# Attention's output: scattered to feature rows by DMA and divided there, in place of two rounds of transposes

## The chip, the cores and the metric

The kernel runs on one core of a Trainium2 chip. The core has a matrix engine (TensorE, "PE" in the profile, with its weight loads as "PEld"), a vector engine (VectorE, "DVE"), a scalar engine (ScalarE, "ACT"), a general engine (GpSimd, "POOL"), and SyncE ("SP"), whose queue issues DMAs. Each engine takes its instructions in program order and waits in that order. The metric is device time in microseconds of one launch; the median of the runs counts.

## The reference, cut to what matters

A sequence of 2048 tokens with 256 features passes through attention, a gated MLP, a second attention, and the same MLP again, each with a layer norm ahead and a residual sum behind. Both attentions are causal and have 16 heads of 16 features; the first has rotary angles and four key heads, the second has 16 key heads. The MLP has 2048 inner features, with weights in 4-bit codes.

```python
probs = softmax(where(causal, q @ k.T * scale, -inf))   # per head, 2048 x 2048
attended = (probs @ v).reshape(S, 256)                  # heads side by side: 16 x 16 features
x = x + attended @ Wo.T + bo                            # the second attention has no bo
x = x + mlp(layernorm(x))
```

The change lies between `probs @ v` and `attended @ Wo.T`.

## The kernel before, in words

Queries are tiled in four blocks `b` of 512 tokens (TB), heads in four groups `g` of four. A unit is one (b, g): 16 units per attention, in the order b = 0: g = 0 to 3, then b = 1, and so on. The number of key tiles grows with the block: 4(b + 1) tiles of 128 keys.

**A unit's main steps** come from `value_steps`. `pair(kt, p)` computes scores with keys on partitions for two heads (L716), adds minus the row maximum (L721) and the mask (L628), and ScalarE takes the exponential (L729). `values(half)` multiplies by V (L703) into one PSUM tile `av`: each of the four heads has 32 rows of it, of which 16 are the output features and row 16 is the softmax sum, since V has a column of ones. `end()` copies `av` to `o` in SBUF on ScalarE (L739).

**A unit's side steps** are woven between the main ones. `max_steps` computes the next unit's scores with queries on partitions (L643) and VectorE takes their maxima (L651); `gather` and `turn` bring them into the form that L721 needs. In g = 0 and g = 1 the preparation of the next block is added (`prep_steps`); in the first attention also the unpacking of the MLP's weights, six steps per unit from block 1 on (`dequant_steps`: a load on SP's queue, L314, a POOL step L328, VectorE steps L339 to L354).

**Division and projection.** `divide` of a unit is the first side step of the next one. Four transposes (L746) turn `o` to tokens on partitions, VectorE takes the reciprocal of the sums (L751) and multiplies (L754) into `att`. At the start of the next block, `out_steps` transposes `att` back to feature rows (`turn`, L775), ScalarE copies it to `aT` (L780), and `project` multiplies with `wo` (L787) and adds to `x` (L792). After the last unit of an attention the divide and the out steps become side steps of the MLP's first block (`left`), woven between its `features` steps (L876 on TensorE, L882 to L887 on the others).

**Order.** Nothing is scheduled automatically: every engine's order is the program's. `weave(main, side, rest=4)` spreads the side list evenly over the main steps but the last four; `blend` merges two lists evenly. PSUM has three score tiles `ps_s`, used in turn by pairs, scores and the MLP's features, one `ps_av` and one `ps_m`, which divides, turns and projections share.

**SP's queue** carries, per unit, the eight DMAs of `load_q` for the unit after next (L614), stores of prepared queries and keys (L535, L539), loads of packed weights, and ahead of each MLP the 2 MB load of the down weights `wd` (L868). `load_q` is emitted at the beginning of a unit, ahead of its weave.

Of the kernel before, what the change touches and what calls it, by code (L numbers as in the profile page):

```python
# [8 lines left out]
F32 = mybir.dt.float32  # L9
# [7 lines left out]
ALU = mybir.AluOpType  # L17
# [3 lines left out]
P = 128  # L21
S = 2048
D = 256
NH = 16
HD = 16
NKV = 4
NG = NH // 4
MLP = 2048
NFC = MLP // P
TB = 512  # L30
NB = S // TB
NT = TB // P
# [23 lines left out]
def blend(a, b):  # L56

    keyed = [((n + 0.5) / len(a), 0, n, f) for n, f in enumerate(a)]
    keyed += [((n + 0.5) / len(b), 1, n, f) for n, f in enumerate(b)]
    return [f for *_, f in sorted(keyed, key=lambda k: k[:3])]  # L60
# [3 lines left out]
def tile_hybrid_layers(  # L64
# [25 lines left out]
    nc = tc.nc  # L90
# [9 lines left out]
    small = ctx.enter_context(tc.tile_pool(name="small", bufs=2))  # L100
    pre = ctx.enter_context(tc.tile_pool(name="pre", bufs=1))
    psum = ctx.enter_context(tc.tile_pool(name="psum", bufs=1, space=PSUM))
    dram = ctx.enter_context(tc.tile_pool(name="dram", bufs=1, space=bass.MemoryType.DRAM))
# [7 lines left out]
    def ps_m():  # L111
        return psum.tile([P, 512], F32, tag="m", name="ps_m")
# [36 lines left out]
    for src, at in ((bq, 0), (bk, D), (bv, D + 64)):  # L149
        n = src.shape[1]  # L150
# [18 lines left out]
    ident = const.tile([P, P], F32, tag="ident", name="ident")  # L169
# [221 lines left out]
    class Attention:  # L391
# [293 lines left out]
        def value_steps(self, b, g):  # L685

            nk = NT * (b + 1)
            held = {"pending": []}

            def values(half):  # L690

                kt, q0, es_ = held["pending"][0]
                few = TB - q0 <= TB // 2
                if half == 1:
                    held["pending"].pop(0)
                    if few:
                        return
                elif kt == 0:
                    held["av"] = ps_av()
                own = slice(q0, TB) if few else slice(*((q0, TB // 2), (TB // 2, TB))[half])  # L700
                for j in range(4):
                    h = g if self.first else 4 * g + j
                    nc.tensor.matmul(  # L703
                        held["av"][32 * j : 32 * j + 32, own],
                        lhsT=self.vv[kt // NT][:, kt % NT, h * VW : h * VW + 32],
                        rhs=es_[j // 2][:, j % 2, own],
                        start=(kt == 0 and half == 0), stop=(kt == nk - 1),
                    )

            def pair(kt, p):  # L710
                q0 = max(0, kt - NT * b) * P
                diagonal = kt >= NT * b
                keys = slice((kt % NT) * P, (kt % NT + 1) * P)
                pt = ps_s()
                for r in range(2):
                    nc.tensor.matmul(  # L716
                        pt[:, r, q0:], lhsT=self.key_rows(kt // NT, g, p, r, keys),
                        rhs=self.qT[b, g][64 * r : 64 * r + 64, p, q0:], start=True, stop=False,
                    )
                for r in range(2):  # L720
                    nc.tensor.matmul(  # L721
                        pt[:, r, q0:], lhsT=sel[64 * r : 64 * r + 64, p, :],
                        rhs=self.mT[b, g][64 * r : 64 * r + 64, q0:],
                        start=False, stop=not diagonal,
                    )
                if diagonal:
                    self.add_mask(pt, 1, q0)
                e = self.wk.tile([P, 2, TB], F32, tag="e", name="e", bufs=4)
                nc.scalar.activation(e[:, :, q0:], pt[:, :, q0:], AF.Exp, scale=QK_SCALE)  # L729
                if p == 0:  # L730
                    held["es"] = [e]
                else:
                    held["pending"].append((kt, q0, held["es"] + [e]))

            def end():
                values(0)
                values(1)
                o = pre.tile([P, TB], F32, tag="o", name="o")
                nc.scalar.copy(o, held["av"])  # L739
                held["o"] = o  # L740

            def divide():
                o = held["o"]
                pt = ps_m()
                for i in range(NT):
                    nc.tensor.transpose(  # L746
                        pt[:, i * P : (i + 1) * P], o[:, i * P : (i + 1) * P], ident
                    )
                heads = pt.rearrange("p (t j c) -> p t j c", t=NT, c=32)
                rec = small.tile([P, NT, 4], F32, tag="rec", name="rec")  # L750
                nc.vector.reciprocal(rec, heads[:, :, :, HD])  # L751
                if g == 0:
                    self.att[b] = pre.tile([P, NT, NG, 4, HD], F32, tag="att", name="att")
                nc.vector.tensor_tensor(  # L754
                    self.att[b][:, :, g], heads[:, :, :, :HD],
                    rec.unsqueeze(3).broadcast_to([P, NT, 4, HD]), ALU.mult,
                )

            steps = []
            for kt in range(nk):  # L760
                for p in range(2):
                    steps.append(lambda kt=kt, p=p: pair(kt, p))
                    if kt:
                        steps.append(lambda p=p: values(p))
            return steps, end, divide

        def out_steps(self, b):
            held = {}

            def turn(n):  # L770
                pt = ps_m()
                for i in range(2):
                    flat = self.att[b][:, 2 * n + i].rearrange("p g j c -> p (g j c)")
                    for c in range(2):
                        nc.tensor.transpose(  # L775
                            pt[:, (2 * i + c) * P : (2 * i + c + 1) * P],
                            flat[:, c * P : (c + 1) * P], ident,
                        )
                aT = pre.tile([P, 2, 2, P], F32, tag="aT", name="aT")
                nc.scalar.copy(aT, pt.rearrange("p (i c t) -> p i c t", i=2, c=2))  # L780
                held[n] = aT

            def project(n):
                po = ps_m()
                for i in range(2):
                    for c in range(2):
                        nc.tensor.matmul(  # L787
                            po[:, i * D : (i + 1) * D], lhsT=held[n][:, i, c, :],
                            rhs=self.wo[:, c, :], start=(c == 0), stop=(c == 1),
                        )  # L790
                to = xt[b][:, 2 * n : 2 * n + 2, :]
                nc.vector.tensor_tensor(  # L792
                    to, po.rearrange("p (i d) -> p i d", i=2), to, ALU.add
                )

            return [lambda n=n, f=f: f(n) for n in range(2) for f in (turn, project)]

        def run(self, extra, beside):


            units = [(b, g) for b in range(NB) for g in range(NG)]
            per_unit = -(-len(extra) // (len(units) - NG))
            late, ahead = [], []
            for n, (b, g) in enumerate(units):
                more = []
                if g == 0 and b > 0:
                    more += self.out_steps(b - 1)
                if g == 0 and b + 1 < NB:
                    ahead = self.prep_steps(b + 1)
                    few = -(-len(ahead) // 2)  # L810
                if n >= NG:
                    more, extra = more + extra[:per_unit], extra[per_unit:]
                if g < 2:
                    more, ahead = more + ahead[:few], ahead[few:]
                if n + 2 < len(units):
                    self.load_q(*units[n + 2])
                steps, turn = [], None
                if n + 1 < len(units):
                    steps, turn = self.max_steps(*units[n + 1])
                else:  # L820
                    more += beside
                side = late + (blend(steps, more) if steps else more)
                steps, end, divide = self.value_steps(b, g)
                weave(steps, side, rest=4)
                if turn:
                    turn()
                end()
                late = [divide]
            return late + [lambda: None] * 2 + self.out_steps(NB - 1)


    class Mlp:
# [89 lines left out]
    at = Attention(True, wqkv_a)  # L922
    with tc.tile_pool(name="wk1", bufs=2) as wk, tc.tile_pool(name="kv1", bufs=1) as kv:
        at.wk = at.qpool = wk
        with tc.tile_pool(name="init", bufs=1) as pool:
# [13 lines left out]
            steps, turn = at.max_steps(0, 0)  # L939
# [5 lines left out]
    at = Attention(False, wqkv_b)  # L945
    with tc.tile_pool(name="kv20", bufs=1, reuse_waits="tile") as kv0, tc.tile_pool(
        name="wk2", bufs=2, reuse_waits="tile"
# [7 lines left out]
        steps, turn = at.max_steps(0, 0)  # L955
# [60 lines left out]
```

## Time and profile before

| | |
|---|---|
| time, median of 3 runs (lowest to highest) | 1926.59 us (1915.77 to 1930.18) |
| the profiled execution, its own time | 1916.85 us |
| its span, from the first to the last instruction | 1914.7 us |
| mean granted TensorE clock | 0.979 |
| TensorE busy | 1829.9 us (96%) |
| VectorE, ScalarE, GpSimd busy | 1109.2, 813.5, 238.0 us (58%, 42%, 12%) |
| DMA queues of SP (q1), share of 16 engines | 8.5% |
| L746 transposes, 128 | 22.2 us busy on TensorE |
| L775 transposes, 64 | 11.1 us busy on TensorE |
| L751 and L754 on VectorE, 32 each | 8.2 and 13.6 us |
| L780 copies on ScalarE, 16 | 9.3 us |
| units' ends (copies `o`): first attention | 69.9 to 646.6 us |
| units' ends: second attention | 1024.7 to 1568.0 us |

The page's first part gives each engine's busy time and its share of the span; the clock row has one digit per fortieth of the span, 9 for nine tenths of full clock or more. In the timeline each row is a run of equal instructions of one engine: start and duration in us, engine, line, operation, output and input tiles, shapes, count, and in brackets the idle time ahead of it and what ended it. The end of a TensorE instruction is modelled and overlaps the next start; starts are what can be subtracted.

### The profile page before, as it was taken

Reading aid. Unit: us, or ns where it says so; the run is one execution under the profiler, and the core shown is the slowest. Engines: PE = TensorE matmul, PEld = TensorE weight load, DVE = VectorE, ACT = ScalarE, POOL = GpSimd, SP = SyncE. Lnnn points to the kernel's source line nnn. Section 1 sums busy time; section 2 is a strip of 40 time slices with the busy share of each in tenths; the row PEclk is TensorE's granted clock in tenths of the full one; section 3 lists DMA queues with packets and bytes.
Section 4 is the critical chain, followed back from the end, with each engine's and each line's share of the span. In section 5 each row is a group of like instructions: output and inputs, shape, how many; then the busy total and the mean of one; then the engine's idle time right before and its main releaser. Section 6 shows DMA issues by size and latency. Waiting matters only on the chain. (4 is left out here: it accounts for less than half of the span.)

```text
span 1914.7 us, 31770 instructions
## 1 busy us (share of the span) xinstructions
PE 1829.9 (96%) x13452; PEld 985.9 (51%) x13452; DVE 1109.2 (58%) x1612; ACT 813.5 (42%) x1069; POOL 238.0 (12%) x433
## 2 busy tenths in 40 slices
PE   5899989999999999999999999999999999999999
PEld 3454444444444456656565545445444444756656
DVE  4556677787776253444444667766867715363443
ACT  1334445465666521222214355556556662131221
POOL 3301311300001011112102010010000001011110
PEclk8879999999999999999999899999999999999999
DMA  4510320301101100002305050050000010000000
GB/s 102 131 45 23 72 46 23 73 23 23 34 23 34 45 6 0 1 0 47 75 1 111 24 100 23 13 100 23 13 13 1 2 46 0 11 1 11 6 6 11
DMA packets 42270, 64.23 MB, mean 34 GB/s; under 512 B 13840, under 2 KB 20880, under 8 KB 41872
## 3 DMA queue, kind: packets, MB, share of 16 engines
q1 hardware_dynamic: 33488, 45.93, 8.5%
q0 software_dynamic: 7680, 15.74, 5.1%
q8 instruction: 106, 1.74, 0.4%
q10 hardware_dynamic: 960, 0.52, 0.1%
q14 instruction: 36, 0.29, 0.1%
HBM read 44.24 MB, written 17.83 MB: 32 GB/s over the span
## 5 line engine op out<-in xcount | busy, mean ns | idle before, releaser
L729 ACT ACTIVATE e<-ps_s 128x1024 f32<-128x1024 f32 (+3 forms) x640 | 571.5, 897 | 457.8 <-PE ps_s L628 227.8
L651 DVE TENSOR_REDUCE mx<-ps_s 128x2 f32<-128x1024 f32 (+3 forms) x640 | 657.9, 1061 | 171.0 <-PE ps_s L643 85.9
L703 PE MATMUL ps_av<-e,v 128*32 128x256 f32 (+1 forms) x4608 | 363.9, 383 | 0.7 <-ACT e L729 0.7
L643 PE MATMUL ps_s<-kT,qT 64*128 64x512 f32 (+3 forms) x1280 | 281.8, 436 | 31.3 <-DVE mx L651 12.2
L716 PE MATMUL ps_s<-qT,kT 64*128 64x512 f32 (+3 forms) x1280 | 289.9, 449 | 11.4 <-DVE mx L651 6.1
L876 PE MATMUL ps_s<-xnT,wg 128*128 128x512 f32 x512 | 242.5, 596 | 0.0
L721 PE MATMUL ps_s<-mT,sel 64*128 64x512 f32 (+3 forms) x1280 | 240.9, 372 | 0.2 <-ACT mT L677 0.2
L876 PE MATMUL ps_s<-xnT,wu 128*128 128x512 f32 x512 | 240.6, 592 | 0.0
L643 PEld LDWEIGHTS ps_s<-kT,qT 64*128 64x128 f32 x1280 | 124.3, 187 | 186.1 <-issue 85.4
L716 PEld LDWEIGHTS ps_s<-qT,kT 64*128 64x128 f32 x1280 | 122.3, 187 | 158.6 <-issue 80.9
L884 DVE TENSOR_TENSOR t<-ps_s,t 128x512 f32<-128x512 f32 x128 | 88.2, 689 | 171.2 <-POOL t L883 169.4
L882 ACT ACTIVATE t<-ps_s 128x512 f32<-128x512 f32 x128 | 76.3, 596 | 249.9 <-PE ps_s L876 249.5
L885 ACT ACTIVATE t<-t 128x512 f32<-128x512 f32 x128 | 80.6, 630 | 201.2 <-DVE t L884 201.2
L703 PEld LDWEIGHTS ps_av<-e,v 128*32 128x32 f32 x4608 | 92.7, 108 | 136.6 <-issue 113.4
L876 PEld LDWEIGHTS ps_s<-xnT,wu 128*128 128x128 f32 x512 | 97.3, 190 | 122.5 <-issue 122.5
L883 POOL TENSOR_SCALAR t<-t 128x512 f32<-128x512 f32 x128 | 79.4, 620 | 577.7 <-ACT t L882 574.9
L876 PEld LDWEIGHTS ps_s<-xnT,wg 128*128 128x128 f32 x512 | 96.2, 192 | 106.4 <-issue 104.5
L886 DVE SCALAR_TENSOR_TENSOR t<-t,ps_s 128x512 f32<-128x512 f32 x128 | 88.1, 688 | 89.0 <-ACT t L885 89.0
L721 PEld LDWEIGHTS ps_s<-mT,sel 64*128 64x128 f32 x1280 | 124.5, 190 | 10.0 <-ACT mT L677 6.5
L628 PE MATMUL ps_s<-mask_t,mask_w 64*128 64x64 bf16 x2048 | 125.1, 199 | 0.0
L901 PE MATMUL ps_av<-wd,inter 128*128 128x256 f32 x512 | 114.5, 380 | 0.0
L901 PE MATMUL ps_m<-wd,inter 128*128 128x256 f32 x512 | 114.3, 380 | 0.0
(123 smaller groups left out, 1188.3 us busy)
## 6 DMA issues: line engine op xcount, KB each, us to landing
qT<-h SPq DMA_DIRECT2D x256, 64.0 KB, 2.3
kT<-h POOLq DMA_DIRECT2D x96, 128.0 KB, 6.1
h<-high SPq DMA_DIRECT2D x24, 256.0 KB, 3.0
h<-low SPq DMA_DIRECT2D x24, 256.0 KB, 3.3
wd<-wd_kept SPq DMA_DIRECT2D x2, 2048.0 KB, 7.8
wd_kept<-dq_d SPq DMA_DIRECT2D x4, 512.0 KB, 2.7
out<-x SPq DMA_DIRECT2D x16, 128.0 KB, 1.7
x<-x SPq DMA_DIRECT2D x3, 512.0 KB, 5.1
```

Of the source, the lines that this page charges most:

```text
L628: nc.tensor.matmul(pt[:, r, to], lhsT=mask_w[rows, kind, part, :], rhs=mask_t[rows, kind, part, :], start=False, stop=(part == 1),)
L643: nc.tensor.matmul(pt[:, r, :w], lhsT=self.qT[b, g][64 * r : 64 * r + 64, p, i * P : (i + 1) * P], rhs=self.key_rows(c, g, p, r, slice(0, w)),
L651: nc.vector.tensor_reduce(held["mx"][:, i, 2 * p : 2 * p + 2, c], pt[:, :, :w], AX.X, ALU.max)
L703: nc.tensor.matmul(held["av"][32 * j : 32 * j + 32, own], lhsT=self.vv[kt // NT][:, kt % NT, h * VW : h * VW + 32], rhs=es_[j // 2][:, j % ...
L716: nc.tensor.matmul(pt[:, r, q0:], lhsT=self.key_rows(kt // NT, g, p, r, keys), rhs=self.qT[b, g][64 * r : 64 * r + 64, p, q0:], start=True ...
L721: nc.tensor.matmul(pt[:, r, q0:], lhsT=sel[64 * r : 64 * r + 64, p, :], rhs=self.mT[b, g][64 * r : 64 * r + 64, q0:], start=False, stop=no ...
L729: nc.scalar.activation(e[:, :, q0:], pt[:, :, q0:], AF.Exp, scale=QK_SCALE)
L876: nc.tensor.matmul(pt[:, k, :], lhsT=w[:, c, fc * P : (fc + 1) * P], rhs=self.xnT[b][:, c, :], start=(c == 0), stop=(c == 1),)
L884: nc.vector.tensor_tensor(t, gate, t, ALU.mult)
L885: nc.scalar.activation(t, t, AF.Tanh, scale=GELU_C)
L886: nc.vector.scalar_tensor_tensor(t, t, 1.0, gate, ALU.add, ALU.mult)
L901: nc.tensor.matmul(po[:, :D], lhsT=inter[:, fc, i * P : (i + 1) * P], rhs=wd[:, fc, :], start=(fc == 0), stop=(fc == NFC - 1),)
```

## The change

`end()` still copies `av` to `o`. Then, on SP's queue, eight DMAs per unit: for each of four heads the 16 feature rows go into `att`, now a tile with features on partitions for two groups (128 rows, 512 tokens, one tile per pair of groups), and the row of 512 sums is cut into 16 rows of 32 in `den`. There is no `divide` for even g. For odd g two side steps follow in the next unit: `invert` takes the reciprocal of `den` (128 x 32) on VectorE, stores it to device memory by one DMA, and loads it back by eight, each head's row of 512 repeated on 16 partitions, into `factor`; `divide` multiplies `att` by `factor` in place. `project` uses `att` as it stands. The transposes L746 and L775, the copies `aT` and the reads of PSUM by L751 and L754 are gone.

The place of these steps changes too: `late` holds `invert` and `divide`, and after g = 3 the two projections; they are inserted at positions 3, 10, 13 and 15 of the next unit's side list. Units with odd g have no such steps. After the last unit all four come first in the MLP's side list.

```diff
@@ -737,24 +737,39 @@
                 values(1)
                 o = pre.tile([P, TB], F32, tag="o", name="o")
                 nc.scalar.copy(o, held["av"])
-                held["o"] = o
+
+
+                if g % 2 == 0:
+                    self.att[b, g // 2] = (
+                        pre.tile([P, TB], F32, tag="att", name="att", bufs=2),
+                        small.tile([P, 32], F32, tag="den", name="den"),
+                    )
+                att, den = self.att[b, g // 2]
+                for j in range(4):
+                    rows = slice(64 * (g % 2) + HD * j, 64 * (g % 2) + HD * (j + 1))
+                    nc.sync.dma_start(out=att[rows], in_=o[32 * j : 32 * j + HD])
+                    nc.sync.dma_start(out=den[rows], in_=o[32 * j + HD : 32 * j + HD + 1])
+
+            def invert():
+                den = self.att[b, g // 2][1]
+                rec = small.tile([P, 32], F32, tag="rec", name="rec")
+                nc.vector.reciprocal(rec, den)
+
+                kept = dram.tile([8, TB], F32, tag="rec", name="rec_kept", bufs=2)
+                nc.sync.dma_start(
+                    out=kept.rearrange("h (s q) -> (h s) q", q=32), in_=rec
+                )
+                factor = pre.tile([P, TB], F32, tag="factor", name="factor")
+                for h in range(8):
+                    nc.sync.dma_start(
+                        out=factor[HD * h : HD * (h + 1)],
+                        in_=kept[h : h + 1].broadcast_to([HD, TB]),
+                    )
+                held["factor"] = factor
 
             def divide():
-                o = held["o"]
-                pt = ps_m()
-                for i in range(NT):
-                    nc.tensor.transpose(
-                        pt[:, i * P : (i + 1) * P], o[:, i * P : (i + 1) * P], ident
-                    )
-                heads = pt.rearrange("p (t j c) -> p t j c", t=NT, c=32)
-                rec = small.tile([P, NT, 4], F32, tag="rec", name="rec")
-                nc.vector.reciprocal(rec, heads[:, :, :, HD])
-                if g == 0:
-                    self.att[b] = pre.tile([P, NT, NG, 4, HD], F32, tag="att", name="att")
-                nc.vector.tensor_tensor(
-                    self.att[b][:, :, g], heads[:, :, :, :HD],
-                    rec.unsqueeze(3).broadcast_to([P, NT, 4, HD]), ALU.mult,
-                )
+                att = self.att[b, g // 2][0]
+                nc.vector.tensor_tensor(att, att, held["factor"], ALU.mult)
 
             steps = []
             for kt in range(nk):
@@ -762,30 +777,16 @@
                     steps.append(lambda kt=kt, p=p: pair(kt, p))
                     if kt:
                         steps.append(lambda p=p: values(p))
-            return steps, end, divide
+            return steps, end, [invert, divide] if g % 2 else []
 
         def out_steps(self, b):
-            held = {}
-
-            def turn(n):
-                pt = ps_m()
-                for i in range(2):
-                    flat = self.att[b][:, 2 * n + i].rearrange("p g j c -> p (g j c)")
-                    for c in range(2):
-                        nc.tensor.transpose(
-                            pt[:, (2 * i + c) * P : (2 * i + c + 1) * P],
-                            flat[:, c * P : (c + 1) * P], ident,
-                        )
-                aT = pre.tile([P, 2, 2, P], F32, tag="aT", name="aT")
-                nc.scalar.copy(aT, pt.rearrange("p (i c t) -> p i c t", i=2, c=2))
-                held[n] = aT
-
             def project(n):
                 po = ps_m()
                 for i in range(2):
+                    t = (2 * n + i) * P
                     for c in range(2):
                         nc.tensor.matmul(
-                            po[:, i * D : (i + 1) * D], lhsT=held[n][:, i, c, :],
+                            po[:, i * D : (i + 1) * D], lhsT=self.att[b, c][0][:, t : t + P],
                             rhs=self.wo[:, c, :], start=(c == 0), stop=(c == 1),
                         )
                 to = xt[b][:, 2 * n : 2 * n + 2, :]
@@ -793,7 +794,7 @@
                     to, po.rearrange("p (i d) -> p i d", i=2), to, ALU.add
                 )
 
-            return [lambda n=n, f=f: f(n) for n in range(2) for f in (turn, project)]
+            return [lambda n=n: project(n) for n in range(2)]
 
         def run(self, extra, beside):
 
@@ -803,8 +804,6 @@
             late, ahead = [], []
             for n, (b, g) in enumerate(units):
                 more = []
-                if g == 0 and b > 0:
-                    more += self.out_steps(b - 1)
                 if g == 0 and b + 1 < NB:
                     ahead = self.prep_steps(b + 1)
                     few = -(-len(ahead) // 2)
@@ -819,14 +818,18 @@
                     steps, turn = self.max_steps(*units[n + 1])
                 else:
                     more += beside
-                side = late + (blend(steps, more) if steps else more)
-                steps, end, divide = self.value_steps(b, g)
+                side = blend(steps, more) if steps else more
+
+                for at, step in zip((3, 10, 13, 15), late):
+                    side.insert(at, step)
+                steps, end, late = self.value_steps(b, g)
                 weave(steps, side, rest=4)
                 if turn:
                     turn()
                 end()
-                late = [divide]
-            return late + [lambda: None] * 2 + self.out_steps(NB - 1)
+                if g == NG - 1:
+                    late += self.out_steps(b)
+            return late
 
 
     class Mlp:
```

## The prediction

> **What bounds the kernel.** I read the page first: engine shares, the clock row, then the groups.
>
> ```profile
> span 1914.7 us, 31770 instructions
> PE 1829.9 (96%) x13452; PEld 985.9 (51%) x13452; DVE 1109.2 (58%) x1612; ACT 813.5 (42%) x1069; POOL 238.0 (12%) x433
> PEclk8879999999999999999999899999999999999999
> qT<-h SPq DMA_DIRECT2D x256, 64.0 KB, 2.3
> ```
>
> TensorE is busy almost throughout, so time that it no longer spends is gained, and any wait put in its program order is paid in full. The timeline of TensorE in attention's last block shows the steady step: scores (L643), a pair's two halves (L716, L721), values (L703), scores again.
>
> ```profile
> 1443.70 0.50 PE L643 MATMUL ps_s<-kT,qT 64*128 64x512 f32 x2
> 1444.04 0.40 PE L716 MATMUL ps_s<-qT,kT 64*128 64x512 f32 x2
> 1444.27 0.39 PE L721 MATMUL ps_s<-mT,sel 64*128 64x512 f32 x2
> 1444.59 0.64 PE L703 MATMUL ps_av<-e,v 128*32 128x256 f32 x8
> 1445.16 0.50 PE L643 MATMUL ps_s<-kT,qT 64*128 64x512 f32 x2
> ```
>
> From start to start 1.46 us: a pair 0.66, values 0.57, scores 0.23 (the first of a kind after another kind 0.1 more). One scores tile keeps VectorE (L651) 1.22 us, one pair keeps ScalarE (L729) 1.02; both fit under 1.46.
>
> **Removed.** The same timeline where one unit ends and the next begins:
>
> ```profile
> 1430.68 0.59 ACT L739 COPY o<-ps_av 128x512 f32<-128x512 f32 x1
> 1430.84 0.49 PE L721 MATMUL ps_s<-mT,sel 64*128 64x512 f32 x2
> 1431.33 0.66 PE L746 MATMUL ps_m<-ident,o 128*128 128x128 f32 x4
> 1431.91 0.50 PE L716 MATMUL ps_s<-qT,kT 64*128 64x512 f32 x2
> ```
>
> L721 would have handed over after 0.23, at 1431.07; with the four transposes the next pair starts at 1431.91: a hole of 0.84 us, partly the wait for the copy `o`. Bounds for its removal: 0.84 if TensorE can use it all; 0.25 if ScalarE's queue (mT, o, then exps of 1.03) holds the first pairs anyway. I take 0.7, since scores tiles can fill the hole. There are 16 divides per attention: 12 in units that follow inside a block, 3 at a block's start, 1 after the last unit.
> - 24 ordinary ones: 24 x 0.7 = 16.8 us.
> - At a block's start divide, turn and turn stand together. Block 2: L721 at 277.17, next pair at 279.77, so 2.37 us lost, and 0.59 for the second turn. Others lack the 0.90 wait in it; I take 2.7 x 6 = 16.2.
> - The two ends of attention (in the MLP's first features): three transpose groups at 0.44, then this wait on ScalarE's aT copy (L780), twice, with what it does to the clock:
>
> ```profile
> 669.81 3.00 PE L787 MATMUL ps_m<-wo,aT 128*128 128x256 f32 x8 [2.81 <-ACT aT L780]
> 672.61 2.60 PE L876 MATMUL ps_s<-xnT,wg 128*128 128x512 f32 x4
> 675.05 1.88 PE L876 MATMUL ps_s<-xnT,wu 128*128 128x512 f32 x4
> 670.00:675.00 5.00, 5.00 (x12) 3.12 (x12) 1.38 (x3) 0.00 (x0) 0.00 (x0) 0.66 0.15 52
> ```
>
> After 2.81 us without work the clock of that stretch is 0.66: the eight L787 take 2.80 instead of 1.72, the next four 2.44 instead of 1.72, so 1.8 us more. Each end returns 1.3 + 2.8 + 1.8 = 5.9, together 11.8.
>
> Credit: 44.8 us. VectorE gives back 32 x (0.26 + 0.43) = 21.9 and takes on 16 x (0.26 reciprocal, by L751; 0.69 product, by L536) = 15.2; ScalarE loses 16 aT copies of 0.58. Neither is the bound: 0.
>
> **Added: a round trip on SP's queue.** Each unit issues 8 DMAs, each second one 9 more: 32 x 8 + 16 x 9 = 400. Of all the work on SP what counts is its order, for SP issues one at a time and waits in order. The nearest row is a load_q, eight DMAs:
>
> ```profile
> 178.79 3.57 SPq L614 DMA_DIRECT2D qT<-h  x8
> ```
>
> They start 0.47 apart and land 2.2 after issue. Let S be the start of the copy `o`. Simpler shapes (L535, L539) issue in 0.33, so I take 0.42 apart for the new ones.
> - o done S+0.6; eight att/den issues to S+4.0; last den landed S+5.7.
> - The next load_q now stands behind them, not ahead of them: S+4.0 to S+7.7. `rec` is ready at S+6.0, but its DMA queues behind load_q.
> - kept issued S+7.7, landed S+9.9 (2.1 by L535); SP waits there, then eight factor issues, the last at S+13.1, landed S+15.2.
> - Product 0.7: VectorE is free at S+15.9, `project` may start at S+16.1 (S+16.5 where dq's load also stands ahead, first attention, blocks 1 and 2).
>
> Here a rule can be weighed. The Trainium skill, "DMA: Bandwidth & Descriptors", section "Issuing engines are not separate DMA queues", says the sequencer's time to start a DMA is usually small beside the DMA. By that the three trips cost 2.1 each and project is ready at about S+7.8. The row says 25 issues in line, 3.6 us per eight against 2.2 for one landing. The same page's "Rules for kernel authors" warns that many small transfers under 64 KB are mostly overhead; that speaks against this change. I go by the row: S+16.
>
> **Who waits.** Inserted at 3, 10, 13, 15 of the side list. I counted what `weave` and `blend` put ahead of each and priced it with 0.66, 0.57, 0.23.
> - TensorE at `project(0)` in blocks 1, 2, 3 (pairs, values, scores ahead). First attention: 5,3,5 = 6.2; 7,4,6 = 8.3; 10,8,9 = 13.2. Second: 6,4,6 = 7.6; 8,5,7 = 9.7; 12,9,11 = 15.6. Waits 10.3, 8.2, 2.9, 8.5, 6.4, 0.5: 36.8 us. Everything on TensorE is queued behind.
> - VectorE at `divide` in units g = 2. Behind it stand L651's maxima, and TensorE stops when the three ps_s tiles are used up; I allow 1.8 us of cover. VectorE arrives at 8.5, 9.7, 11.2 (first), 10.8, 12.0, 12.7 (second), and is free at 15.9: 5.6 + 4.4 + 2.9 + 3.3 + 2.1 + 1.4 = 19.7; block 0 of the second attention, whose unit is over after 12.4, 1.7 more. 21.4.
> - The wait at `invert` (S+5.7) lies before these same stops and is in them.
> - dq's load in units g = 1, blocks 1 and 2: now issued S+7.7, landed 3.0 later, unpacked by POOL 0.6: S+11.4, where VectorE (L339) wanted it at S+6.2 and S+6.4. 5.1 less 1.8, twice: 6.6.
> - The two ends: VectorE reaches invert after the first feature's chain, S+7.9; kept goes behind the 2 MB load of wd (issued S+4.0, 7.8 us to land); factor lands between S+15.6 and S+17.3; TensorE has done two features (3.44 each) at S+6.9 and waits till about S+17.2. 10.3 each, 20.6.
> - Clock: 13 of these stops are at least 2.8 us long; 1.8 each by the rows above: 23.4. The skill ("TensorE: Matmul & The Clock Gate", "Part 1: The HAM clock gate") ties half clock to an idle window of 3.4 us. Here it also comes without one: the clock reads 0.50 from 1075 to 1090 after idle pieces of under 0.8 us each. By the rule two or three of the 13 would be free (5 us less); by that row a stop could cost 5 or more. I keep 1.8, and use the rest for the range.
>
> Debit 108.8, credit 44.8: +64 us. On the profiled execution's 1916.9 that is 1981. The median of the runs shown, 1926.6, lies 10 above it; I put half of that on: **1986 us**.
>
> **Rivals.**
> 1. The trip is short and hidden (the skill's reading). Project ready at S+7.8: 1.6 us at one block, none at VectorE's stops; at the ends VectorE still arrives at S+7.9, so 13 - 6.9 = 6.1 twice and 3.6 of clock: debit 17.5, net -27: **1895**. For it: landings of 2.1. Against: 3.57 us for eight issues. It is decided at readiness near S+12: each microsecond of trip costs about 13 us (5 blocks, 6 VectorE stops, 2 ends).
> 2. The ps_s tiles cover VectorE's stops. Then 21.4, 6.6 and the clock of six stops (10.8) go: +25, **1947**. For it: scores run ahead a whole unit. Against: L643 already waits on L651 in block 0.
> 3. The clock stays halved longer, as from 1075 to 1090: 4 us more at 12 stops, **2034**.
>
> **Numbers.** Forecast 0.48, rival 1 0.11, rival 2 0.20, rival 3 0.15, near no change otherwise 0.06. Ends of unknown costs: divide holes 0.25 to 0.84 (-11 to +3 us), trip 2.5 shorter (-35) to 2 longer (+28), clock. I give 1935 to 2045. One per cent is about what this measurement can tell from no change. Slower by over that: 0.48 + 0.15 + 0.12 of rival 2 + 0.03 = 0.78; within: 0.11; faster 0.11.
>
> **What would show it.** No L746 or L775; TensorE's waits list L787 behind the product on VectorE, six times inside attention with up to 10 us and twice at the ends; VectorE's waits name DMA factor for 14 stops and DMA den for short ones; SP shows kept behind qT; the clock row has more digits under 9. I am wrong if factor lands before S+12, or if the idle time before L651 grows but TensorE's does not.

## The result, and the profile after

The changed kernel takes **2024.28 us** (median of 4 runs, 2022.18 to 2024.62) against 1925.08 us before, also of 4 runs: 1.0519 times as long, 95% interval 1.0477 to 1.0560. It is slower by 99 us. The forecast was 1986 us with a range of 1935 to 2045: the sign and the mechanism were right, the size was low by 38 us. Rival 3, the clock that stays halved for longer, had 2034 and lies nearer.

The page after, the lines that answer to the first four shown of before:

```profile
span 2022.7 us, 32014 instructions
PE 1850.6 (91%) x13260; PEld 985.8 (49%) x13260; DVE 1103.3 (55%) x1580; ACT 804.4 (40%) x1053; POOL 237.2 (12%) x433
PEclk8778898899999989999999789899999998999999
qT<-h SPq DMA_DIRECT2D x256, 64.0 KB, 2.3
```

TensorE's count fell by the 192 transposes, yet it is busy 20.7 us longer, and its share fell from 96 to 91%. From these lines the 108.0 us by which the span grew can be split. Time in which TensorE did nothing (span less busy) went from 84.8 to 172.1 us: 87.3 us more. Busy time lost 33.3 us of transposes (the two groups' 22.2 and 11.1) and still rose by 20.7, so what remained ran 54.0 us longer. The granted clock fell from 0.979 to 0.945, which is 40 against 111 us of full clock missing from the span. In the traces' clock record, which knows only 1.00 and 0.50, TensorE was busy for 64.9 us at half clock before and for 164.6 after; half of the difference is 49.9 us, so the clock explains nearly all of the 54.0. Of the debit some three fifths are waits and two fifths a slower TensorE.

TensorE's waits in the changed kernel (total us, times, longest):

```profile
PE ps_m L788 <- DVE att L772: 43.4, 8, 13.0
PE ps_s L716 <- DVE mx L651: 33.8, 27, 5.7
PE ps_s L643 <- ACT e L729: 20.0, 37, 1.2
PE ps_s L643 <- DVE mx L651: 10.1, 24, 2.0
```

Before, the last three were 6.1, 6.4 and 12.2 us. L788 is the projection, L772 the product by `factor`. And what VectorE waits for in the same kernel; only the third was there before, with 1.3 us:

```profile
DVE att L772 <- DMA factor<-rec_kept: 81.3, 16, 11.6
DVE rec L756 <- DMA den<-o: 37.6, 14, 5.0
DVE dq_t L339 <- POOL dq_b L328: 40.4, 6, 10.9
```

The trip itself, from the timeline of the first block change of the first attention (start, duration, engine):

```profile
145.34 0.59 ACT L739 COPY o<-ps_av 128x512 f32<-128x512 f32 x1
145.96 0.51 SPq L750 DMA_DIRECT2D att<-o  x1
146.51 0.59 SPq L751 DMA_DIRECT2D den<-o  x1
...
151.59 3.79 SPq L614 DMA_DIRECT2D qT<-h  x8
152.64 0.35 DVE L756 RECIPROCAL rec<-den 128x32 f32<-128x32 f32 x1 [4.96 <-DMA den<-o]
155.47 0.37 SPq L314 DMA_DIRECT2D dq_q<-gate_p  x1
155.94 0.38 SPq L759 DMA_DIRECT2D rec_kept<-rec  x1
158.48 3.57 SPq L764 DMA_DIRECT2D factor<-rec_kept  x8
163.86 0.69 DVE L772 TENSOR_TENSOR att<-att,factor 128x512 f32<-128x512 f32 x1 [2.13 <-DMA factor<-rec_kept]
164.60 1.65 PE L788 MATMUL ps_m<-wo,att 128*128 128x256 f32 x3 [6.13 <-DVE att L772]
```

The reciprocals are ready at 153.0 and their store is issued at 155.94, behind eight load_q and a load of packed weights. From the start S of the copy to the product 18.5 us pass: 13.6 of them SP issuing one DMA after another, 4.0 the landings of the store and of the last `factor` load, the rest the copy and small gaps.

### The profile page after: what moved, and what is told of

It reads as the page before. It is cut to its first block, busy times and chain, and to the rows that moved or that the text cites. A ratio compares the mean times of both kernels' runs of the same rounds, so it can differ in the third digit from the quotient of the medians.

```text
span 2022.7 us, 32014 instructions
## 1 busy us (share of the span) xinstructions
PE 1850.6 (91%) x13260; PEld 985.8 (49%) x13260; DVE 1103.3 (55%) x1580; ACT 804.4 (40%) x1053; POOL 237.2 (12%) x433
## 5 line engine op out<-in xcount | busy, mean ns | idle before, releaser
L703 PE MATMUL ps_av<-e,v 128*32 128x256 f32 (+1 forms) x4608 | 373.1, 394 | 1.8 <-ACT e L729 1.8
L716 PE MATMUL ps_s<-qT,kT 64*128 64x512 f32 (+3 forms) x1280 | 301.9, 462 | 43.2 <-DVE mx L651 33.8
L643 PE MATMUL ps_s<-kT,qT 64*128 64x512 f32 (+3 forms) x1280 | 293.9, 451 | 42.5 <-ACT e L729 20.0
L721 PE MATMUL ps_s<-mT,sel 64*128 64x512 f32 (+3 forms) x1280 | 249.5, 380 | 0.2 <-ACT mT L677 0.2
L643 PEld LDWEIGHTS ps_s<-kT,qT 64*128 64x128 f32 x1280 | 132.3, 195 | 204.1 <-issue 93.4
L716 PEld LDWEIGHTS ps_s<-qT,kT 64*128 64x128 f32 x1280 | 126.5, 192 | 204.9 <-DVE mx L651 85.7
L721 PEld LDWEIGHTS ps_s<-mT,sel 64*128 64x128 f32 x1280 | 131.5, 196 | 9.2 <-ACT mT L677 6.5
```

Source lines behind the costliest of these rows:

```text
L643: nc.tensor.matmul(pt[:, r, :w], lhsT=self.qT[b, g][64 * r : 64 * r + 64, p, i * P : (i + 1) * P], rhs=self.key_rows(c, g, p, r, slice(0, w)),
L703: nc.tensor.matmul(held["av"][32 * j : 32 * j + 32, own], lhsT=self.vv[kt // NT][:, kt % NT, h * VW : h * VW + 32], rhs=es_[j // 2][:, j % ...
L716: nc.tensor.matmul(pt[:, r, q0:], lhsT=self.key_rows(kt // NT, g, p, r, keys), rhs=self.qT[b, g][64 * r : 64 * r + 64, p, q0:], start=True ...
L721: nc.tensor.matmul(pt[:, r, q0:], lhsT=sel[64 * r : 64 * r + 64, p, :], rhs=self.mT[b, g][64 * r : 64 * r + 64, q0:], start=False, stop=no ...
```

## Experiments

Theory: engines wait in program order behind a round trip that SP issues one by one, and TensorE's clock falls behind each stop. Rivals: the DMAs cost by themselves (traffic, ports); each stop costs a fixed spell of clock whatever its length; the stops are only moved. Every kernel below is the changed kernel with the edit shown. Each ratio is to runs of the kernel before on the same chip. The differences named in the text are between medians; by the ratios they can be up to 6 us smaller.

| run | edit | median us | ratio to before, 95% interval |
|---|---|---|---|
| the change | | 2024.3 | 1.0519, 1.0477 to 1.0560 |
| x1_const | nobody waits for factor | 1943.7 | 1.0106, 1.0065 to 1.0148 |
| x2_credit | no added DMAs at all | 1870.3 | 0.9727, 0.9686 to 0.9768 |
| x3_loadq | load_q behind factor | 1985.2 | 1.0323, 1.0278 to 1.0368 |
| x4_tail | the two ends later | 1998.9 | 1.0378, 1.0314 to 1.0441 |
| x5_dq | dq_q on ScalarE's queue | 1996.0 | 1.0400, 1.0365 to 1.0435 |
| x6_late | blocks' products later | 1981.9 | 1.0319, 1.0285 to 1.0352 |
| x9_const_dq | x1_const and x5_dq | 1914.6 | 0.9969, 0.9951 to 0.9988 |
| x7_warm | filling matmuls in the waits | 2015.7 | 1.0485, 1.0458 to 1.0511 |
| x10_b0 | load_q later in two units | 2015.6 | 1.0502, 1.0458 to 1.0545 |
| x12_den_only | one den load for four | 1983.1 | 1.0323, 1.0265 to 1.0381 |
| x8_all | x3 to x6 together, x10's idea in most units without a reciprocal | 1899.0 | 0.9894, 0.9863 to 0.9925 |
| x11_den1 | x8_all and x12's edit | 1875.1 | 0.9764, 0.9738 to 0.9790 |

**x1_const: the waits for factor.**

```diff
-                nc.vector.tensor_tensor(att, att, held["factor"], ALU.mult)
+                nc.vector.tensor_tensor(att, att, flat, ALU.mult)
```

`flat` is a tile of ones, set once; attention's output stays undivided.

> The product takes a tile of ones in place of factor, so the output is not divided; every DMA is still issued and the reciprocal is still taken. Theory (waits in program order behind SP's round trip): the waits for factor go, which the prediction put at 36.8 us (projections), 21.4 us (VectorE at divide), some 16 us at the two ends, and the halved clock behind them, 20 us or more. 1905 to 1925 us, about the time of before or a little under; TensorE idle near before's, no wait for factor. Rival (the 400 DMAs themselves cost: issue time, traffic, shared ports): the DMAs are all still there, so it stays above 1990 us.

1943.7 us: 81 us of the 154 between the change and x2_credit are waits for factor. Neither had its number right: the theory's was 19 us too low, the rival's bound 46 too high. What stays is told by this kernel's own wait (L341 is L339, moved by two lines):

```profile
DVE dq_t L341 <- POOL dq_b L330: 42.2, 7, 10.8
DVE rec L758 <- DMA den<-o: 36.7, 14, 4.2
```

**x2_credit: the gain alone.** The bodies of the scatter, `invert` and `divide` are left out, and:

```diff
-            return steps, end, [invert, divide] if g % 2 else []
+            return steps, end, [lambda: None] * 2 if g % 2 else []
-                            po[...], lhsT=self.att[b, c][0][:, t : t + P],
+                            po[...], lhsT=flat[:, t : t + P],
```

> All the added DMAs, the reciprocal and the product are left out; the projections take a tile of ones, so attention's output is left out. Only the removal of transposes and of their copies remains. Theory: the credit of the prediction, 44.8 us under before: about 1880 us (lower end of the divide's hole, 0.25 us each: 1891). Rival (ScalarE's exponentials hold the units' beginnings, so the hole is not used): 1905 or more. The difference to x1_const is what the DMAs cost while nobody waits for factor: about 20 us by the theory (dq's load behind SP's queue, short waits for den), 100 us by the rival of x1_const.

1870.3 us, 48.9 us under before: the predicted credit was 44.8. That ScalarE's exponentials hold the holes closed is refuted. Its page:

```profile
span 1866.7 us, 31296 instructions
PE 1790.5 (96%) x13260; PEld 962.0 (52%) x13260; DVE 1090.5 (58%) x1548; ACT 804.2 (43%) x1053; POOL 238.5 (13%) x434
```

The difference to x1_const is 73 us, not 20: a second debit beside the waits for factor.

**x9_const_dq and x5_dq: the queue's other customers.**

```diff
-                nc.sync.dma_start(out=q, in_=src) if ...
+                nc.scalar.dma_start(out=q, in_=src) if ...
```

> x1_const (the product takes ones, so the output is not divided; all DMAs issued) with dq_q on ScalarE's queue as well. x1_const less x2_credit is 73 us, of which 37 lie in four units of the first attention, blocks 1 and 2, g = 0 and 1. Theory: those are VectorE waiting for packed weights, so 37 us go: about 1907 us. Rival (traffic or issue of the added DMAs): no change, 1944.

> The changed kernel with one edit: the loads of packed weights (dq_q, twelve of them) are issued on ScalarE's queue instead of SP's, where they stood behind att, den and load_q. Theory as predicted: VectorE's wait for the unpacked codes goes, 6.6 us and two halved spells of 1.8: about 2014 us. Theory as x1_const mended it (the queue holds these loads back some 10 us in blocks 1 and 2, in four units): the two units with g = 1 give back 18 us, those with g = 0 stay bound by factor: about 2004 us. Rival (traffic of the added DMAs): no change, 2024.

x9 takes 1914.6 us, 29 less than x1_const. x5 takes 1996.0, 28 less than the change and more than both sizes expected. The traffic is the same in all of them, so what counts is the place on SP's queue. VectorE's wait at L339 in x5_dq:

```profile
  POOL dq_b L328: 6.4, 2
```

40.4 us have become 6.4. In the change's unit (1, 1) the packed weights are issued 10.5 us after S (before: 2.4), and VectorE stands 9.8 us at L339.

**x3_loadq: the slope.**

```diff
-                if n + 2 < len(units):
+                if n + 2 < len(units) and not late:
                     self.load_q(*units[n + 2])
...
+                if n + 2 < len(units) and late:
+                    side.insert(4, lambda u=units[n + 2]: self.load_q(*u))
```

> In the units that invert, load_q is issued right behind the loads of factor instead of ahead of the store of the reciprocals. The trip becomes 3.7 us shorter. Theory: each microsecond of trip costs about 13 us, so 48 us less than the changed kernel: about 1976 us; factor lands near S+13.5 instead of S+17; the two ends are as before. Rival (what costs is that TensorE stops at all, each stop throwing the clock into a halved spell of fixed length): stops get shorter but stay, so no more than 15 us less: about 2009.

1985.2, 39 us less. The last factor load is issued 3.5 us earlier (medians S+12.6 against S+16.0), so a microsecond of trip is worth at most 11 us; 13 was predicted, 4 by the rival. At most, because in the units with g = 0 the packed weights move forward as well (in (1, 0) from S+10.1 to S+6.4), and VectorE's wait at L339 falls from 40.4 to 31.2 us. TensorE's waits:

```profile
PE ps_m L788 <- DVE att L772: 35.0, 6, 13.1
PE ps_s L716 <- DVE mx L651: 18.9, 20, 5.9
```

**x4_tail: the two ends.**

```diff
                     if b + 1 < NB:
-                        side += self.prep_steps(b + 1)
+                        side = side[:1] + self.prep_steps(b + 1) + side[1:]
```

> At the two ends the product and the projections come behind the next block's layer norm and transposes in the MLP's side list (some 40 us later), the reciprocal stays first. Theory: two stops of 13 us on TensorE and their halved clock (about 3 us each) go: 30 us less than the changed kernel, about 1994 us, and no wait for the product there. Rival (VectorE's work is only put off and TensorE stops later for it): 10 us less or nothing.

1998.9, 25 us less: the two waits of 13.0 and 12.8 us are gone (the longest at L788 is now 6.5) and nothing stops later for them: the waits at L716 and L643 stay as they were.

**x6_late: the blocks.** Where `late` is inserted:

```diff
-                for at, step in zip((3, 10, 13, 15), late):
-                    side.insert(at, step)
+                if (b, g) == (0, 2):
+                    side.insert(3, late[0])
+                    carried = late[1]
+                elif (b, g) == (0, 3):
+                    side.insert(8, carried)
+                elif late:
+                    at = int(len(side) * {2: (0.0, 0.9, 0.6, 0.45), 0: (0.0, 0.62, 0.5, 0.42)}[g][b])
+                    for k, step in zip((3, at, at + 3, at + 5), late):
+                        side.insert(k, step)
```

> The changed kernel with the product and the projections of a block put later in the side list, by shares of the unit so that they come some 18 us or more after the unit's begin; the reciprocal stays at position 3, the ends stay as they are. Theory: the waits for factor inside attention go. All waits for factor are worth 81 us (the changed kernel less x1_const), the two ends 30 of them: 50 us less, about 1974 us. Rival (VectorE and TensorE only stop elsewhere, since the wait of SP holds up load_q and the rest of the queue): above 2005.

1981.9, 42 us less, 8 short of the theory. At L788 little more than the two waits of the ends is left (25.6 us in 3), and the waits for den and packed weights stay too.

**x10_b0: a collision that nobody had priced.** The unit (0, 1) of each attention inverts nothing and still grew, from 32.1 to 37.4 and from 23.1 to 28.4 us.

```diff
-                if n + 2 < len(units):
+                if n + 2 < len(units) and n != 1:
...
+                if n == 1:
+                    side.insert(len(side) // 2, lambda u=units[3]: self.load_q(*u))
```

> The changed kernel with one edit: in the unit (block 0, g = 1) of each attention load_q is issued half way through the side list instead of at the unit's begin. That unit has no reciprocal, yet it grew by 5.3 us in each attention. Theory: att, den and load_q hold back the store of the prepared keys on SP's queue, GpSimd waits for it in load_k, and its sum (L501), ScalarE's copy and VectorE's subtraction stand behind: with load_q out of the way the unit gets 3 to 4 us shorter in each attention and some clock comes back: 7 to 12 us less, about 2014 us. Rival (these units are longer for the clock or for ps_m): no change, 2024.

The units are back at 32.9 and 23.0 us. Of the 10 us gained there 4.6 are lost again in the units behind them, (0, 2), which take 16.5 and 18.1 instead of 14.3 and 15.7; the span is 8.7 us shorter, and where the rest of that comes from was not traced. By the ratio the gain is inside the intervals; by the timeline the cause of the unit's growth is plain. First the changed kernel, then x10_b0:

```profile
82.09 0.47 SPq L535 DMA_DIRECT2D h<-high  x1
84.92 4.09 POOL L601 DMA_DIRECT2D kT<-h  x8 [8.66 <-DMA h<-high]
89.03 1.27 POOL L501 TENSOR_TENSOR r<-r 128x512 f32<-128x512 f32 x1
90.34 0.62 ACT L528 CAST high<-r 128x512 fp32r<-128x512 f32 x1 [7.53 <-POOL r L501]
```

```profile
77.29 0.54 SPq L535 DMA_DIRECT2D h<-high  x1
80.18 4.11 POOL L601 DMA_DIRECT2D kT<-h  x8 [4.77 <-DMA h<-high]
84.31 1.28 POOL L501 TENSOR_TENSOR r<-r 128x512 f32<-128x512 f32 x1
```

SP's queue holds back the store of the keys (issued at 82.09 instead of 77.29), and GpSimd waits for it in load_k. The sum (L501) that ScalarE, VectorE and then TensorE need stands behind load_k's eight DMAs on GpSimd; TensorE waits 6.85 us for it at L481.

**x7_warm: the clock by itself.**

```diff
                 po = ps_m()
+                for k in range({3: 14, 0: 5}.get(b, 0) if n == 0 else 0):
+                    nc.tensor.matmul(po, lhsT=ident, rhs=wqkv_b[:, 0, :TB], start=True, stop=True)
```

> The changed kernel with filling matmuls ahead of the first projection: 14 at each of the two ends and 5 in block 1 of each attention (N = 512, two passes of 0.43 us each: 12.0 and 4.3 us at full clock), written to the projection's PSUM tile, which the projection then starts afresh. They fill time in which TensorE waited (13.0, 12.8, 6.1, 4.5 us), so the waits for factor stay as long. Theory (the halved clock behind a wait is a cost of its own): the spells at 720, 1170 to 1184 and 1679 us and most of that at 153 go; their busy time is 5.9, 8.9, 5.7 and 9.8 us, half of it lost, so up to 15 us less: 2009 to 2015 us, with TensorE's clock near 1.00 behind the ends. Rival (the clock follows from something else, or the filling costs what it saves): 2024 or more.

2015.7, 8.6 us less; the intervals of the two ratios overlap, so the time alone would not settle it. The stretches at the first end do: first the changed kernel, then this one (stretch, PE, PEld, DVE, ACT, POOL busy, granted clock, DMA).

```profile
720.00:725.00 5.00, 0.00 (x0) 0.00 (x0) 0.00 (x0) 0.00 (x0) 0.00 (x0) 0.50 0.22 41
725.00:730.00 5.00, 2.44 (x6) 2.00 (x7) 2.46 (x4) 0.63 (x1) 0.00 (x0) 0.50 0.08 20
730.00:735.00 5.00, 5.00 (x10) 2.24 (x9) 0.90 (x2) 0.00 (x0) 0.00 (x0) 0.65 0.00 0
```

```profile
720.00:725.00 5.00, 4.09 (x13) 2.17 (x12) 1.29 (x2) 0.37 (x1) 0.00 (x0) 1.00 0.20 39
725.00:730.00 5.00, 5.00 (x17) 2.89 (x16) 1.97 (x3) 0.86 (x2) 0.24 (x1) 1.00 0.00 0
730.00:735.00 5.00, 5.00 (x15) 2.53 (x14) 2.67 (x4) 1.23 (x2) 0.46 (x2) 1.00 0.15 52
```

The projection still comes after the product, but the clock stays at 1.00. From the last copy `o` of the first attention to the first of the second the time falls from 387.7 to 384.7 us, from the last of the second to the end from 356.1 to 353.3, and in the two units of block 1, g = 0, from 47.9 to 44.8 and from 41.9 to 40.2. So the halved clock is a cost of its own: about 10 us in these four places, by the two profiled executions.

**x12_den_only: four loads in one.**

```diff
+                half = slice(64 * (g % 2), 64 * (g % 2) + 64)
+                nc.sync.dma_start(out=den[half], in_=o[HD:P:32])
                 for j in range(4):
                     rows = ...
                     nc.sync.dma_start(out=att[rows], in_=o[32 * j : 32 * j + HD])
-                    nc.sync.dma_start(out=den[rows], in_=o[32 * j + HD : 32 * j + HD + 1])
```

> The changed kernel with the four den loads of a unit made into one and issued first; all places as in the changed kernel. SP's queue gets 1.9 us shorter per unit (3 issues of 0.63 us), so factor lands and dq_q is issued 1.9 us earlier. Theory: x3_loadq gave 39 us for 3.8 us of trip, 10 per us: 19 us less, and 4 more for dq_q in two units: about 2001 us. Rival (only the wait for den itself is shortened, and that lies under cover): 2020 or more.

1983.1, 41 us less, where the theory had 23. The waits for den are gone from VectorE's list, those for factor are down from 81.3 us:

```profile
DVE att L773 <- DMA factor<-rec_kept: 67.4, 15, 9.5
```

The span fell by 42.9 us: 24.4 of it TensorE's idle time (172.1 to 147.7), 18.5 its busy time at a better clock (0.945 to 0.956). The likely reason for the other 18 us is VectorE's stop at `invert`, which the prediction had counted into the later stops; no run takes away this stop alone. x9_const_dq speaks for it: where nothing waits for factor any more, and for packed weights hardly, 44 us are still left above x2_credit, and the longest wait there for an added DMA is that for den, 36.2 us in 13.

**x8_all and x11_den1: all mends.** x8_all joins x4, x5 and x6, and issues load_q behind factor or a third into the side list; x11_den1 adds the single den load.

> All mends together: product and projections late, at the ends behind the next block's preparation; load_q behind the loads of factor or a third into the side list; dq_q on ScalarE's queue. Every value is computed as in the changed kernel. Theory: what is left is x2_credit's 1870 us and some short waits for den: 1875 to 1895 us, faster than before by 1.5 to 2.5%. Rival (400 DMAs cost by themselves): no faster than before, 1920 or more.

> x8_all with the four den loads of a unit made into one, issued ahead of att, from four partitions 32 apart. Three issues of 0.63 us per unit less on SP and den landed by about S+3.5 instead of S+7. Theory: the waits for den (34 us on VectorE in x8_all, mostly under cover) go, and in block 0, where x8_all still stands 20 us above x2_credit, the queue is shorter: 5 to 12 us less than x8_all, about 1890 us. Rival (those waits are covered already, block 0 is bound by VectorE and the clock): 1899, no change.

1899.0 and **1875.1 us**: the latter computes every value of the changed kernel, beats the kernel before by 2.4%, and stands 5 us above x2_credit, which issues none of the added DMAs. The page of x11_den1:

```profile
span 1873.6 us, 31869 instructions
PE 1796.1 (96%) x13260; PEld 963.9 (51%) x13260; DVE 1101.4 (59%) x1580; ACT 804.3 (43%) x1053; POOL 238.3 (13%) x433
PEclk8879999999999999999999999999999999999999
```

That the DMAs cost much by themselves is refuted: 304 of the 400 are still there, with the same bytes, and some 5 us are all that is left for them. In x11_den1 no wait of VectorE for factor or den is left over, and TensorE waits 1.9 us for the product. x8_all lies 4 us above the range expected, and x11 was expected at 1890; of the 24.7 us of span between x8_all and it 16.1 are TensorE's busy time, that is clock: 0.973 in x8_all, 0.984 here.

## Why the prediction was right, and where its sizes were off

- **Sign and mechanism: right.** Waits in program order behind SP's round trip outweigh the removed transposes. x1_const, x3_loadq, x4_tail and x6_late each give back some four fifths of what was expected of the waits named, and x11_den1 keeps the credit once the waits are gone.
- **The debit in two parts.** By their pages the changed kernel's TensorE is idle for 95.9 us more than x2_credit's, where waits of 85.4 were predicted, and busy for 60.1 us more with the same 13260 matmuls, where 23.4 us of clock were. The waits were sized within an eighth; the clock was not.
- **Credit, 44.8: right.** 48.9 by x2_credit. One step of the sum does not follow from its lines: by them a block's start gives 2.96 us with the wait of 0.90 at L775 and 2.06 without, and the trace before has that wait at three of the six, which makes 15.1 us instead of 16.2.
- **The trip, S+15.2 for the last factor: short by 2 to 3 us.** Over half of that is the 0.42 us between issues of att and den. They take 0.587 each and start 0.63 apart, so eight take 5.1 us instead of 3.4; den is there at S+7.3, not S+5.7. The order behind it (load_q, dq's load, kept) came as described.
- **Where engines stop: right in sum, wrong in place.** 36.8 in the blocks' projections, 20.6 at the ends and 28.0 elsewhere were predicted, 85.4 in all. Measured: 17.6 in the blocks and 25.8 at the ends, both at L788, and at L716 and L643 behind VectorE and the exponentials 39.2 more than before (33.8 + 20.0 + 10.1 less 6.1, 6.4 and 12.2): 82.6. That the sums agree so closely is luck, since the places miss by 5 to 19 us. In blocks TensorE mostly stops for a scores tile before it reaches the projection, since VectorE is already standing at `invert`, at `divide` or before the packed weights.
- **dq's load, 6.6: too small.** Seen rightly as a mechanism, priced in two units with an issue at S+7.7. In (1, 1) it stood at S+10.5; VectorE waited 5 to 11 us in five units, and x5_dq gave back 28 us.
- **The wait at `invert` "is in" the later stops: by all signs wrong.** x12_den_only gave 41 us where 23 were expected from the trip and dq; the stop itself was not isolated.
- **The store of keys in (0, 1): not seen**, though SP's stores were in the list of what the queue carries: 10.6 us in the two units, of which x10_b0 keeps about half one unit later.
- **The clock, 23.4: the largest miss.** It took 1.8 us per stop from one stop of 2.8 us, and counted 13. The busy time shows 54.0 against before. The clock record has 25 halved spells in the changed kernel, 221.8 us together, and 6 before, 78.5 us: more of them than stops counted, and 8.9 us long on average, so that one costs up to 4.4 us. One that follows a gap of 3.10 us at L716 lasts 17.07 us, with TensorE busy throughout:

```profile
1255.70:1259.10 3.40, 1.23 (x18) 0.60 (x18) 3.11 (x4) 0.43 (x1) 0.00 (x0) 1.00 0.00 0
1259.10:1276.17 17.07, 17.07 (x127) 9.38 (x126) 8.69 (x11) 7.07 (x11) 0.00 (x0) 0.50 0.03 7
```

  That is rival 3's mechanism, to which the prediction gave 0.15. x7_warm shows that the clock has its own price at the long stops; how much of the rest comes from many short gaps was not separated.
- **The rule weighed, DMA starts: the row was right.** By the Trainium skill's sentence ("DMA: Bandwidth & Descriptors", "Issuing engines are not separate DMA queues") the trip was 7.8 us; it was over 18. 25 issues in line, 0.42 to 0.63 us from one to the next, make most of the trip; the landings, 1.7 to 2.4 us each, make some 4.

## What to carry to other kernels

Price a step moved to DMA by the issues in line on its queue, and look at everything that now stands behind them: here waiting for the trip cost 81 us, the packed weights 28 and another engine's keys some 5, while for the traffic itself some 5 are left. A consumer in program order must be placed by measured time after its producer, not by a count of steps; the same DMAs placed later, fewer and on another queue turned 5% slower into 2.4% faster. On a busy TensorE a wait can cost twice: once while it lasts, once in the clock behind it.

## What the runs showed of the hardware that was not expected

A DMA of 16 rows from SBUF to SBUF held SP for 0.59 us (att and den alike, 32 KB and 2 KB), longer than the store of 128 rows (0.37, rec_kept) and the broadcast load from memory (0.42, factor): an issue is not priced by its bytes. In the traces' clock record the halved spells last 3.41 us or multiples of it (up to 34.1 in x8_all), which is the window that the Trainium skill names ("TensorE: Matmul & The Clock Gate", "Part 1: The HAM clock gate"). By the rule there, half clock comes after an idle window and full clock after a busy one. Neither holds here as it stands. In the changed kernel TensorE was busy for 0 to 2.46 us of the 3.41 us ahead of each of the 25 spells, and for none of it only at the two ends; in unit (1, 1) the clock halves from 207.8 to 218.0 us, from the last part of a gap of 2.97 on. And it stays halved under load: in the stretch of 17.07 us shown above, and in x8_all from 1048.5 to 1082.6 with TensorE busy 32.7 of these 34.1 us (by the profile's modelled ends). So short gaps are not free. What decides stays open: other stretches of 3.41 us with 1.6 to 2.3 us of work are not followed by half clock.
